# First attention products of two chunks moved into the last superchunk's LSTMs, with the pieces around them placed anew

## Chip, cores and metric

The kernel runs on one core of a Trainium2 chip, in one launch. The metric is the device time of that launch in microseconds (us). Before the change it was 1873.44 us, the median of three runs (1873.34 to 1873.54).

## What is computed

The input is x, 128 batches of 64 tokens with 256 channels, in f32. Four layers each add to x something made of relu(layernorm(x)). Layer 0 is a graph convolution with two products and batch norms. Layer 1 is two graph convolutions, and then LSTMs over windows of 1, 2, 3 and 4 tokens. Layer 2 is a causal attention with one head, layer 3 an attention with four heads and a mask. Cut to what matters here:

```python
# layer 1, with h = relu(layernorm(x))
h = relu(einsum('ts,bsh->bth', adj, h @ Wg0 + bg0))
h = relu(einsum('ts,bsh->bth', adj, h @ Wg1 + bg1))
for p in range(1, 5):                      # windows of p tokens, an LSTM over each
    last = lstm(Wih[p-1], Whh[p-1], bih[p-1], bhh[p-1], windows(h, p))
    h = h with token (p-1) of each window set to last
x = x + h
# layer 2, with h = relu(layernorm(x))
q, k, v = split(h @ Wqkv)
attn = softmax(causal(q @ k.T / 16 + adj))
x = x + (attn @ v) @ Wo
```

## The kernel before

The 8192 tokens are cut into 16 chunks of 512, and for the LSTMs two chunks make a superchunk, so there are 8 superchunks, numbered 0 to 7. The stages follow each other: layer 0; then, at `START`, the convolutions of chunks 0 and 1 with the first pieces of chunk 2; then the LSTMs of the eight superchunks one after the other; then the two attentions, chunk by chunk.

The order of the instructions on TensorE, VectorE, GpSimd and the DMA queue of SyncE (and, from the LSTMs on, on ScalarE) is the order of the program. Each engine works through its own list, and waits at an instruction until what it needs is there.

**The LSTMs.** `lstms(sc, hT)` is a generator that runs `single` (windows of one token) and then `lstm` for p = 2, 3, 4, and yields at places in between. The loop at the end of the stage counts the places: `single` ends at place 3, p = 2 takes 4 to 7, p = 3 takes 8 to 13, p = 4 takes 14 to 21; halves (4.5, 5.5) are places within a step. Each matrix product is done in seven block products, called by their kinds 1 to 7. In `single` the kinds stand in the order 2, 1, 5, 6, 3, 7, 4 for three gates each; kinds 1, 6, 7 and 4 go to the same three PSUM banks, so a product into them waits until VectorE (L1386) or ScalarE has taken the one before. The VectorE helper lines that come up again are L1386 (adds in `single`), L1378 (its new state), L1134 (adds at the start of `lstm`), L1104 (the state l_hs of a step), L298 (`add_squares`).

**What runs beside them.** At each place the loop takes the next piece of other generators, in the order in which `units` put them there:

- `convolutions(c)` for the chunks of the next superchunk, and, begun earlier still, for those of the one after it. It has 16 pieces: (1) scale, on VectorE; (2) transposes on VectorE (L1002), a store of the result to HBM, four loads of it in another order, and the load of x; (3) `add_squares`, which adds what was loaded to x; (4, 5) sums for the norm on VectorE and GpSimd; (6, 7) its application on ScalarE; (8) aggregation on TensorE; (9) two copies on VectorE; (10) the product v, 3.4 us on TensorE; (11) bound on VectorE; (12) the product u, 3.5 us on TensorE; (13) bias on VectorE; (14) aggregation; (15, 16) relu on ScalarE. Two pieces of chunk 2 run in `START`.
- `residual(c)` for the chunks of the superchunk before: transposes on VectorE (L1302) and a store; four loads; `add_squares`.
- `ahead(c)` for chunks whose residual is done: a reordering through HBM, norm, and a store of relu(layernorm(x)) for layer 2.

The tuples `FIRST` and `BEGUN` (superchunk 0), `CONV` (1 to 6), `RESIDUAL`, `LATE`, `LATEST`, `AHEAD` and `FINAL` say at which place each piece of the two chunks stands. In superchunk 0 the first tuple of `FIRST` is for chunk 2, the second for chunk 3; those of `BEGUN` are for chunks 4 and 5.

**Superchunk 7** has no convolutions beside it. Where TensorE would idle there, `IDLE` puts `keep_busy`: transposes of the identity matrix that nobody reads (L151), 54 of them in five places. At place 8 the loads of the first two chunks for layer 2 are issued.

**The attentions.** A hand-written list of steps, `FIRST` (a second variable of that name), begins them: `q2` and `v2a`, `v2b` are the first products of layer 2, `score2`, `exp2`, `divide2`, `turn2`, `out2` its attention, `keep` stores x, `norm3`, `apply3`, `chan3` make the channel-major input of layer 3, `q30` to `k31` and `v3a`, `v3b` its products, `score3` its scores. `res1` are the three pieces of `residual` and `pair1` the reordering for the last two chunks, 14 and 15, whose LSTMs have just ended. After `FIRST` come the lists `THIRD`, `ROUND`, `NORM` and `LAST`.

```python
n = -1
for mark in lstms(sc, hTs[sc]):
    n = n + 0.5 if mark else int(n) + 1
    for u in todo.pop(n, ()):
        next(u)
```

Of the kernel before, what the change touches and what calls it, by code (L numbers as in the profile page):

```python
# [8 lines left out]
F32 = mybir.dt.float32  # L9
# [10 lines left out]
def kernel(  # L20
# [841 lines left out]

    xs = {}
    w1, close_w1 = pool("w1", 1)
    l1, close_l1 = pool("l1", 2)
    l1r, close_l1r = pool("l1r", 2, "right")
    wg0_sb = w1.tile([P, KD, D], F32, name="wg0_sb")
    wg1_sb = w1.tile([P, KD, D], F32, name="wg1_sb")
    nc.sync.dma_start(wg0_sb, wg0.rearrange("(k p) f -> p k f", p=P))
# [5 lines left out]

    wih1 = w1.tile([P, 3, 7, P], F32, name="wih1")

    def load_single():

        rest = l1.tile([P, KD, CH], F32, tag="cell", name="wih1_rest", bufs=1)[:, 0, : 3 * P]  # L880
        rest = rest.rearrange("p (g f) -> p g f", g=3)
        for g, q in enumerate(GATES[:3]):
            raw = wih_t[0].rearrange("(k p) (q f) -> p k q f", p=P, f=D)[:, :, q]
            nc.sync.dma_start(wih1[:, g, 0], raw[:, 0, :P])
            nc.sync.dma_start(rest[:, g], raw[:, 0, P:])
            nc.sync.dma_start(wih1[:, g, 1:3], raw[:, 1].rearrange("p (c f) -> p c f", c=KD))
        yield
        w = wih1.rearrange("p g s f -> p s g f")
        for dst, a, b, op in ((3, rest, w[:, 2], OP.add), (4, w[:, 3], w[:, 0], OP.subtract),
                              (5, w[:, 0], rest, OP.subtract), (6, w[:, 1], w[:, 4], OP.subtract)):  # L890
            nc.gpsimd.tensor_tensor(w[:, dst], a, b, op)
        yield
# [15 lines left out]
    def scaled(y, c, m):  # L908
# [4 lines left out]
        else:  # L913
            nc.vector.tensor_scalar(y[:, m, :], z2[c][:, m, :], sc2[:, one], sh2[:, one],
                                    op0=OP.mult, op1=OP.add)

    def conv_tile(c):

        t = l1.tile([P, KD * CH], F32, tag="cv", name=f"cv_{c}", bufs=2)
        return t.rearrange("p (k n) -> p k n", k=KD), t.rearrange("p (j d) -> p j d", d=D)  # L920
# [417 lines left out]
    def single(b, name, t, ending):  # L1338
# [21 lines left out]
        def product(kind):  # L1360
            for g in range(3):
                nc.tensor.matmul(folded(ps(g, kind)), wih1[:, g, KINDS1[kind], :], right[kind],  # L1362
                                 start=kind in (2, 5, 1), stop=True, skip_group_check=True)
# [143 lines left out]

    RESIDUAL = (0, 3, 5.5), (2, 5, 8.5)
    CONV = (3, 4, 5, 5.5, 7, 8, 9, 10, 10), (5, 5, 6, 9.5, 11, 11.5, 13, 14, 15, 15.5, 17, 18, 20)
    BEGUN = (11, 11, 14.5, 17, 17, 20, 21), (17.5, 19, 21)  # L1510
    FIRST = (1, 1, 1, 2, 3, 4, 4, 5, 5.5, 7, 8, 9, 10, 10), (1, 2, 4.5, 5, 5, 6, 9.5, 11, 11.5, 13, 14, 15, 15.5, 17, 18, 20)
    AHEAD = (6, 7), (9, 10)
    LATE = (4.5, 4.5, 5.5, 9, 19.5), (9, 9.5, 11, 12, 21)
    LATEST = (4.5, 4.5, 5.5, 9, 9.5), (9.5, 9.5, 10, 11, 11.5)
    IDLE = {5: 4, 7: 18, 9: 10, 13: 14, 15: 8}
    FINAL = (6, 7, 11, 11, 12, 15, 15.5), (9, 10, 13, 13, 16, 17, 17.5)
# [25 lines left out]
    with tc.manual_schedule(engines={mybir.EngineType.PE, mybir.EngineType.DVE, mybir.EngineType.Pool,  # L1542
# [4 lines left out]
        for sc in range(last + 1):  # L1547
# [22 lines left out]
            if sc + 1 < last:  # L1570
                for i in range(SUP):
                    units(BEGUN[i], convs[(sc + 2) * SUP + i])
            n = -1
            for mark in lstms(sc, hTs[sc]):
                n = n + 0.5 if mark else int(n) + 1
                for u in todo.pop(n, ()):
                    next(u)
                if sc == last and n in IDLE:
                    keep_busy(IDLE[n], f"l{n}")
                if sc == last and n == 8:  # L1580

                    new_hT(sc + 1)
                    for c in range(SUP):
                        load2(c, hTs[sc + 1][:, c, :].rearrange("p (q n) -> p q n", q=Q))
            assert not todo
# [4 lines left out]

    w2p, close_w2 = pool("w2", 1)
    l2, close_l2 = pool("l2", 2)
    wqv_sb = w2p.tile([P, KD, 2 * D], F32, name="wqv_sb")
    nc.sync.dma_start(wqv_sb, products_far)
    wqk_sb, wvo_sb = wqv_sb[:, :, :D], wqv_sb[:, :, D:]
    w3_sb = w2p.tile([P, KD, 3 * D], F32, name="w3_sb")
    nc.sync.dma_start(w3_sb, w3.rearrange("(k p) f -> p k f", p=P))

    def project_v(dst, hT, w, first, name, pairs=range(NJ // 2)):
        for t in pairs:  # L1600
            ps = bank(f"v_{name}_{t}").rearrange("p (j d) -> p j d", d=D)
            for i in range(2):
                j = 2 * t + i
                for k in range(KD):
                    nc.tensor.matmul(ps[:, i, :], hT[:, k, j, :], w[:, k, first : first + D], start=(k == 0),  # L1605
                                     stop=(k == KD - 1))
            nc.scalar.copy(dst[:, 2 * t : 2 * t + 2, :], ps)  # L1607

    def project_t(m, hT, w, name):
        ps = bank(f"p{m}_{name}")  # L1610
        for k in range(KD):
            nc.tensor.matmul(ps.rearrange("p (a n) -> p a n", n=P), w[:, k, m * P : (m + 1) * P],  # L1612
                             hT[:, k], start=(k == 0), stop=(k == KD - 1))
        return ps


# [41 lines left out]
    for l in "23":  # L1658
# [6 lines left out]
    steps["load2"] = lambda c: load2(  # L1665
        c, l2.tile([P, Q, CH * KD // Q], F32, tag="hT2", name=f"hT2_{c}"))


    @step
    def q2(c):  # L1670
        st[c, "q2"] = q = l2.tile([P, KD, CH], F32, tag="q", name=f"q2_{c}")
        hT = st[c, "hT2"]
        nc.scalar.copy(q[:, 0, :], project_t(0, hT, wqk_sb, f"q2_{c}"))
        st[c, "q2b"] = project_t(1, hT, wqk_sb, f"q2_{c}")

# [4 lines left out]
    def v2h(c, t):  # L1680
        if not t:
            st[c, "v2"] = l2.tile([P, NJ, D], F32, tag="v", name=f"v2_{c}")
        project_v(st[c, "v2"], st[c, "hT2"], wvo_sb, 0, f"2_{c}", [t])

# [260 lines left out]

    @step
    def table(c):

        nc.scalar.activation(small.tile([P, 1], F32, tag="table", name="table"),
                             hTs[last][:, 0, :1], AF.Exp)  # L1950
# [57 lines left out]
    def store(c, t):  # L2008
# [3 lines left out]
        for r in range(2):  # L2012
# [18 lines left out]

    FIRST = """table+0 load2+2 q2+0 copyq2+0 res1+14 res1+15 v2a+0 v2b+0 score2+0 res1+14 res1+15
               exp2+0 q2+1 divide2+0 copyq2+1 load2+3 turn2+0 v2a+1 v2b+1 out2+0 keep+0 res1+14 res1+15
               score2+1 norm3+0 exp2+1 q2+2 divide2+1 copyq2+2 apply3+0 back+0 v2a+2 v2b+2 turn2+1
               score2+2 chan3+0 pair1+14 pair1+14 out2+1 keep+1 exp2+2 divide2+2 q30+0 k30+0 turn2+2
               norm3+1 pair1+15 pair1+15 q31+0 k31+0 apply3+1 out2+2 keep+2 square3+1 score3+0 norm3+2
               v3a+0 load3+1 v3b+0"""
    LAST = """exp3-2 sum3-2 load3+0 divide3-2 qa-1 q5-1 c11-1 v3a-1 qb-1 c12-1 qc-1 turn3-2 qd-1 out3-2
# [26 lines left out]
    close_l2()  # L2065
    close_w2()
    close_l3()
# [47 lines left out]
```

## Time and profile before

The page is of one profiled execution, of 1871.9 us from the first to the last instruction. The stages that the change touches, from the table of busy times by window:

| Stage | window, us | TensorE busy, us | VectorE busy, us |
|---|---|---|---|
| end of START and first half of superchunk 0 | 265 to 340 | 71.82 | 45.04 |
| rest of 0, and superchunks 1 to 6 (most) | 440 to 1360 | 915.94 | 662.40 |
| superchunk 7 | 1360 to 1505 | 138.47 | 97.37 |
| start of the attentions | 1505 to 1560 | 54.29 | 37.30 |
| end of the attentions | 1700 to 1872 | 166.23 | 123.20 |

A row of the profile's groups reads: line, engine, operation, what it writes, what it reads, size, how often; then busy time and the mean of one; then how long the engine idled just before such instructions, and who released it. The granted clock of TensorE stands beside each window: 1.00 is full speed.

The 54 transposes of `IDLE` are recorded at 0.272 us each, and overlap: 18 in a row take 2.13 us, so one takes up 0.118 us.

### The profile page before, as it was taken

The numbers are of one execution on the slowest core, as the hardware profiler recorded it, in microseconds if no ns is written. First come the engines' busy times: TensorE is split into PE (matmuls) and PEld (weight loads), VectorE is DVE, ScalarE is ACT, GpSimd is POOL, SyncE is SP. The second block draws the span as 40 slices with busy tenths as digits, with TensorE's granted clock in tenths as the row PEclk, the third lists the DMA queues.
The fourth block names the chain that finished last, engine by engine and source line by source line (L and its number), as shares of the span: only waits on it lengthen the run. The fifth ranks groups of instructions, "written<-read, shape, count | busy, mean of one in ns | idle before, by whom it ended". The sixth has DMA issues, their size and how long they took to land.

```text
span 1871.9 us, 40786 instructions
## 1 busy us (share of the span) xinstructions
PE 1839.2 (98%) x15509; PEld 1513.0 (81%) x15509; DVE 1322.3 (71%) x3410; ACT 1051.9 (56%) x2500; POOL 614.1 (33%) x856
## 2 busy tenths in 40 slices
PE   8999989999999999999999999999999999999998
PEld 6877856996997898799699689789969967777776
DVE  6768856667677667777866866876667667766776
ACT  5766635556557466565655655746555534444453
POOL 5855723223213323222322332332222214322232
PEclk9999999999999999999999999999999999999999
DMA  3223642224333333341432532342234244444433
GB/s 115 71 68 136 236 184 65 84 98 158 124 114 145 115 136 125 112 157 49 158 130 108 181 124 114 147 136 103 96 102 153 68 158 138 154 140 141 142 114 114
DMA packets 113010, 234.48 MB, mean 125 GB/s; under 512 B 11696, under 2 KB 76592, under 8 KB 112816
## 3 DMA queue, kind: packets, MB, share of 16 engines
q1 hardware_dynamic: 111920, 230.02, 36.5%
q8 instruction: 123, 2.02, 0.4%
q0 software_dynamic: 320, 1.05, 0.2%
q10 hardware_dynamic: 576, 0.82, 0.1%
q14 instruction: 71, 0.58, 0.1%
HBM read 164.21 MB, written 67.63 MB: 124 GB/s over the span
## 4 chain that ended last, share of the span: by engine, by line
PE 83%; DVE 9%; ACT 3%; POOL 2%; issue 1%; DMA 1%; SPq 0%; DVEq 0%; ACTq 0%; POOLq 0%
PE x L1180 22%; PE z L1180 11%; PE y L1180 5%; PE v L1605 5%; PE y L1127 4%; PE u L943 3%; PE v L929 3%; PE p_q L1612 3%; PE x L1362 3%; PE y L1362 3%; PE X L1801 3%; PE x L1127 2%; PE X L437 2%; PE X L513 2%; PE z L1127 1%
## 5 line engine op out<-in xcount | busy, mean ns | idle before, releaser
L1095 ACT ACTIVATE l_gates<-l_gates,bias 128x256 f32<-128x256 f32 (+4 forms) x528 | 238.1, 498 | 211.9 <-DVE l_gates L1189 110.1
L1180 PE MATMUL x<-xd,wset 128*128 128x128 f32 (+2 forms) x1152 | 255.0, 303 | 0.2 <-ACT l_gates L1186 0.2
L1180 PE MATMUL x<-l_hd,wset 128*128 128x128 f32 (+2 forms) x1152 | 254.5, 303 | 0.0
L1246 POOL TENSOR_TENSOR l_gates<-l_gates 128x512 f32<-128x512 f32 (+2 forms) x48 | 75.2, 1567 | 386.4 <-ACT l_gates L1095 386.4
L1189 DVE TENSOR_TENSOR l_gates<-l_gates,z 128x128 f32<-128x128 f32 (+2 forms) x384 | 102.5, 319 | 130.8 <-PE z L1180 128.8
L1180 PEld LDWEIGHTS x<-xd,wset 128*128 128x128 f32 x1152 | 187.7, 191 | 5.9 <-issue 0.5
L1180 PEld LDWEIGHTS x<-l_hd,wset 128*128 128x128 f32 x1152 | 187.8, 191 | 5.0
L1189 DVE TENSOR_TENSOR l_gates<-l_gates,x 128x128 f32<-128x128 f32 (+2 forms) x384 | 121.3, 321 | 91.9 <-PE x L1180 88.2
L1180 PE MATMUL z<-l_hs,wset 128*128 128x128 f32 (+2 forms) x768 | 147.2, 304 | 3.7 <-DVE l_hs L1104 3.7
L1180 PE MATMUL z<-hT,wset 128*128 128x128 f32 (+2 forms) x768 | 146.2, 303 | 0.0
L1186 ACT COPY l_gates<-y 128x128 f32<-128x128 f32 (+2 forms) x192 | 53.1, 290 | 137.3 <-PE y L1180 130.7
L1180 PEld LDWEIGHTS z<-l_hs,wset 128*128 128x128 f32 x768 | 116.8, 191 | 9.4 <-DVE l_hs L1104 6.1
L1180 PEld LDWEIGHTS z<-hT,wset 128*128 128x128 f32 x768 | 117.1, 191 | 3.3
L1095 ACT ACTIVATE l_gates<-x,bias 128x128 f32<-128x128 f32 (+2 forms) x216 | 84.9, 393 | 30.8 <-PE x L1180 28.1
L1180 PE MATMUL x<-hT,wset 128*128 128x128 f32 (+2 forms) x384 | 85.9, 305 | 0.0
L1180 PE MATMUL x<-l_hs,wset 128*128 128x128 f32 (+2 forms) x384 | 84.8, 303 | 0.0
L327 POOL TENSOR_TENSOR xd<-hT 128x128 f32<-128x128 f32 (+2 forms) x72 | 42.8, 594 | 128.1 <-DVE hT L1106 100.0
L1180 PE MATMUL y<-l_hd,wset 128*128 128x128 f32 (+2 forms) x384 | 83.5, 310 | 0.3 <-DVE l_hd L327 0.2
L1180 PE MATMUL y<-xd,wset 128*128 128x128 f32 (+2 forms) x384 | 81.9, 305 | 0.9 <-ACT l_gates L1095 0.6
L1620 POOL TENSOR_TENSOR s<-s,mx 128x256 f32<-128x256 f32 (+2 forms) x33 | 40.4, 1226 | 128.4 <-DVE mx L1619 120.6
L1261 ACT ACTIVATE l_gates<-l_cell 128x256 f32<-128x256 f32 (+2 forms) x144 | 55.2, 383 | 42.9 <-DVE l_cell L1260 42.9
L1607 ACT COPY v<-v 128x512 f32<-128x512 f32 x64 | 37.1, 582 | 71.2 <-PE v L1605 71.1
(350 smaller groups left out, 4588.4 us busy)
## 6 DMA issues: line engine op xcount, KB each, us to landing
wset<-wfar SPq DMA_DIRECT2D x96, 896.0 KB, 6.9
hT<-far_h SPq DMA_DIRECT2D x124, 128.0 KB, 3.2
far_h<-hm SPq DMA_DIRECT2D x16, 512.0 KB, 3.0
far_n<-xs SPq DMA_DIRECT2D x16, 512.0 KB, 3.9
xs<-far_n SPq DMA_DIRECT2D x64, 128.0 KB, 3.8
far_x<-xs SPq DMA_DIRECT2D x16, 512.0 KB, 2.9
x<-far_x SPq DMA_DIRECT2D x64, 128.0 KB, 3.2
xt<-in_x_dram SPq DMA_DIRECT2D x15, 512.0 KB, 3.9
```

The lines of the kernel that those rows point to most:

```text
L929: nc.tensor.matmul(banks[m], wg0_sb[:, k, m * P : (m + 1) * P], agg[:, k, :], start=(k == 0), stop=(k == KD - 1))
L943: nc.tensor.matmul(banks[j // 2][:, j % 2, :], v[:, k, j * P : (j + 1) * P], wg1_sb[:, k, :], start=(k == 0), stop=(k == KD - 1))
L1095: nc.scalar.activation(gate(q, c, part), src, AF.Tanh if q == 2 else AF.Sigmoid, bias=bs[:, q * KD + c : q * KD + c + 1])
L1127: nc.tensor.matmul(folded(self.psum(kind)), wsets[p, self.q][:, BLOCKS[kind][0], :], ox[0][kind], start=kind in (1, 5), stop=True, skip_gr ...
L1180: nc.tensor.matmul(folded(self.psum(kind)), wsets[p, self.q][:, BLOCKS[kind][i], :], (ox[self.s] if part == "x" else oh)[kind], start=firs ...
L1189: nc.vector.tensor_add(gate(self.q, *dst), gate(self.q, *a), self.psum(kind))
L1246: nc.gpsimd.tensor_mul(gates[:, 0, :, :n], gates[:, 0, :, :n], gates[:, 2, :, :n])
L1261: nc.scalar.activation(gate(2, c, part), cells[:, c, part], AF.Tanh)
L1362: nc.tensor.matmul(folded(ps(g, kind)), wih1[:, g, KINDS1[kind], :], right[kind], start=kind in (2, 5, 1), stop=True, skip_group_check=True)
L1605: nc.tensor.matmul(ps[:, i, :], hT[:, k, j, :], w[:, k, first : first + D], start=(k == 0), stop=(k == KD - 1))
L1612: nc.tensor.matmul(ps.rearrange("p (a n) -> p a n", n=P), w[:, k, m * P : (m + 1) * P], hT[:, k], start=(k == 0), stop=(k == KD - 1))
L1801: nc.tensor.matmul(st[c, tag][:, i * CH // 2 : (i + 1) * CH // 2].rearrange("p (a n) -> p a n", n=P), w, st[c, "o7"][kind], start=first an ...
```

## The change

It does three things, which belong together.

1. The first products of layer 2 for chunk 0 (`q2`, `v2`) and chunk 1 (`q2`) are made in superchunk 7, in a new generator `begin_attention` with eight pieces at the places `EARLY`, in place of most of the filler transposes. Of these 8 remain, at a new place, 11. `FIRST` of the attentions loses those steps and is ordered anew.
2. For that, weights and some buffers must live longer than the LSTM stage. A pool `lasting` holds `wg0_sb` and `wg1_sb` (which are loaded anew with the products of layer 2's weights at place 0 of superchunk 7), two chunk-sized buffers `cv`, and four of the seven blocks of `wih1`, whose room then serves v of chunk 0, and after it the weights of layer 3, `w3_sb`, now loaded by a step `weights3`.
3. Pieces are placed anew: those of the residual, and the first late piece of the norm, one place later; those of superchunk 0 spread over later places, with a tuple of its own, `BEGUN_FIRST`, for the chunks begun there.

```diff
-    wg0_sb = w1.tile([P, KD, D], F32, name="wg0_sb")
-    wg1_sb = w1.tile([P, KD, D], F32, name="wg1_sb")
+    wg0_sb = lasting.tile([P, KD, D], F32, name="wg0_sb")
+    wg1_sb = lasting.tile([P, KD, D], F32, name="wg1_sb")
...
+    def begin_attention():
+
+        tiles = [shared(f"{n}2_0") for n in ("hT", "q")]
+        for w, i in ((wg0_sb, 0), (wg1_sb, 1)):
+            nc.sync.dma_start(w, products_far[:, :, i * D : (i + 1) * D])
+        load2(0, tiles[0].rearrange("p (q n) -> p q n", q=Q))
...
+        yield
+        for m in range(KD):
+            nc.scalar.copy(st[0, "q2"][:, m, :], project_t(m, st[0, "hT2"], wg0_sb, "q2_0"))
+            yield
+        for t in range(NJ // 2):
+            project_v(st[0, "v2"], st[0, "hT2"], wg1_sb, 0, "2_0", [t])
+            yield
+        new_hT(last + 1)
+        load2(1, hTs[last + 1][:, 1, :].rearrange("p (q n) -> p q n", q=Q))
+        st[1, "q2"] = hTs[last + 1][:, 0, :].rearrange("p (k n) -> p k n", k=KD)
+        yield
+        for m in range(KD):
+            nc.scalar.copy(st[1, "q2"][:, m, :], project_t(m, st[1, "hT2"], wg0_sb, "q2_1"))
+            yield
+
-    RESIDUAL = (0, 3, 5.5), (2, 5, 8.5)
+    EARLY = 0, 3, 5, 7, 9, 9, 13, 15
+    RESIDUAL = (0, 4, 5.5), (3, 5, 9)
     CONV = (3, 4, 5, 5.5, 7, 8, 9, 10, 10), (5, 5, 6, 9.5, 11, 11.5, 13, 14, 15, 15.5, 17, 18, 20)
     BEGUN = (11, 11, 14.5, 17, 17, 20, 21), (17.5, 19, 21)
-    FIRST = (1, 1, 1, 2, 3, 4, 4, 5, 5.5, 7, 8, 9, 10, 10), (1, 2, 4.5, 5, 5, 6, 9.5, 11, 11.5, 13, 14, 15, 15.5, 17, 18, 20)
+    BEGUN_FIRST = (12, 14.5, 17, 19, 19, 20, 21), (20, 21, 21)
+    FIRST = (1, 3, 3, 4, 4.5, 5, 5.5, 7, 8, 9, 9.5, 11, 11.5, 11.5), (2, 5, 8.5, 9, 9.5, 10, 11, 13, 14, 15, 15.5, 17, 17.5, 19, 20, 20)
     AHEAD = (6, 7), (9, 10)
-    LATE = (4.5, 4.5, 5.5, 9, 19.5), (9, 9.5, 11, 12, 21)
+    LATE = (4.5, 4.5, 5.5, 9, 19.5), (9.5, 9.5, 11, 12, 21)
     LATEST = (4.5, 4.5, 5.5, 9, 9.5), (9.5, 9.5, 10, 11, 11.5)
-    IDLE = {5: 4, 7: 18, 9: 10, 13: 14, 15: 8}
+    IDLE = {11: 8}
...
-                    units(BEGUN[i], convs[(sc + 2) * SUP + i])
+                    units((BEGUN if sc else BEGUN_FIRST)[i], convs[(sc + 2) * SUP + i])
+            if sc == last:
+                units(EARLY, begin_attention())
...
-    FIRST = """table+0 load2+2 q2+0 copyq2+0 res1+14 res1+15 v2a+0 v2b+0 score2+0 res1+14 res1+15
-               exp2+0 q2+1 divide2+0 copyq2+1 load2+3 turn2+0 v2a+1 v2b+1 out2+0 keep+0 res1+14 res1+15
-               score2+1 norm3+0 exp2+1 q2+2 divide2+1 copyq2+2 apply3+0 back+0 v2a+2 v2b+2 turn2+1
-               score2+2 chan3+0 pair1+14 pair1+14 out2+1 keep+1 exp2+2 divide2+2 q30+0 k30+0 turn2+2
-               norm3+1 pair1+15 pair1+15 q31+0 k31+0 apply3+1 out2+2 keep+2 square3+1 score3+0 norm3+2
-               v3a+0 load3+1 v3b+0"""
+    FIRST = """table+0 load2+2 score2+0 res1+14 v2a+1 v2b+1 res1+15 exp2+0 score2+1 divide2+0 q2+2 copyq2+2
+               exp2+1 turn2+0 divide2+1 load2+3 v2a+2 v2b+2 out2+0 keep+0 weights3+0 res1+14 res1+15 turn2+1
+               norm3+0 score2+2 out2+1 keep+1 res1+14 res1+15 exp2+2 apply3+0 back+0 divide2+2 chan3+0
+               pair1+14 pair1+14 turn2+2 q30+0 k30+0 norm3+1 pair1+15 pair1+15 out2+2 keep+2 q31+0 k31+0
+               apply3+1 square3+1 score3+0 norm3+2 v3a+0 load3+1 v3b+0"""
```

## The prediction

> **What bounds it now.** I read the busy shares first, then a table by stage, then the gaps of TensorE one by one. The page:
>
> ```profile
> PE 1839.2 (98%) x15509; PEld 1513.0 (81%) x15509; DVE 1322.3 (71%) x3410; ACT 1051.9 (56%) x2500; POOL 614.1 (33%) x856
> PE 83%; DVE 9%; ACT 3%; POOL 2%; issue 1%; DMA 1%; SPq 0%; DVEq 0%; ACTq 0%; POOLq 0%
> ```
>
> TensorE (PE) is busy 98% and carries 83% of the chain that ended last: a microsecond counts if TensorE idles, or runs dummy transposes, less. The table by stage (PE busy is the second number after the window):
>
> ```profile
> 265.00:340.00 75.00, 71.82 (x441) 49.80 (x440) 45.04 (x96) 40.00 (x80) 19.12 (x23) 0.98 0.25 86
> 440.00:1360.00 920.00, 915.94 (x6871) 783.97 (x6870) 662.40 (x1839) 545.27 (x1424) 261.17 (x374) 1.00 0.36 124
> 1360.00:1505.00 145.00, 138.47 (x887) 121.88 (x886) 97.37 (x292) 83.07 (x222) 37.90 (x59) 1.00 0.32 99
> 1505.00:1560.00 55.00, 54.29 (x492) 36.86 (x491) 37.30 (x90) 23.63 (x45) 14.67 (x19) 1.00 0.58 178
> ```
>
> So 3 us of idle lie in the first superchunk (265 to 340), 4 in the six middle ones, 6.5 in the last (1360 to 1505), and under 1 in the start of the attention. Where, the timeline of PE shows (start, duration, work, in brackets the idle before it and who ended it):
>
> ```profile
> 293.26 4.51 PE L1362 MATMUL x<-xd,wih 128*128 128x512 f32 x6 [2.34 <-DVE l_gates L1386]
> 606.91 1.10 PE L1127 MATMUL y<-hT,wset 128*128 128x256 f32 x4 [0.20 <-DVE hT L1378]
> 656.39 1.41 PE L1180 MATMUL z<-l_hs,wset 128*128 128x168 f32 x8 [0.42 <-DVE l_hs L1104]
> 1406.07 2.13 PE L151 MATMUL idle_l<-ident 128*128 128x128 f32 x18
> ```
>
> The first is one hole; the next two recur in each middle superchunk; the last is a filler, 0.118 us a transpose. Who bounds the start of the attention, the chain of waits tells:
>
> ```profile
> 1516.74 0.12 issue
> 1516.88 0.29 issue
> 1517.17 0.57 DVE xs L1729
> 1517.77 2.49 DVE xs L298 x4
> ...
> 1524.76 0.08 DVE nmr_n L185
> 1524.89 0.48 issue
> 1525.37 1.57 ACT h L187 x3
> 1526.94 0.95 ACT v L1607 x2
> 1527.88 0.28 ACT att L1643
> 1528.21 1.10 PE o L1726 x32
> ```
>
> PE looks full here, but from 1516.7 to 1528 the chain runs through VectorE (DVE) and ScalarE: PE is only just covered. That is the line I trust most.
>
> **The Trainium skill.** (1) "TensorE: Matmul & The Clock Gate", Part 1: the array's clock is halved after an idle window of about 3.4 us and restored after a busy one. The trace agrees: after the 2.34 us hole the granted clock is 0.50 from 293.3 to 296.7, and six matmuls took 4.34 us instead of 2.57 (+1.7). (2) Same page, "Architectural detail": "ACT/DVE are strict FIFO". Here too: the 2.34 us hole is an add behind ten queued pieces of convolution. (3) "DMA: Bandwidth & Descriptors", "Anatomy of one DMA": a fixed cost of about 2 us, mostly the receipt of the last byte. The trace: a 512 KB store of `ym` lands 2.6 to 4.3 us after issue, a 128 KB load of it about 3.1.
>
> **First superchunk, inside.** At place 1 DVE loses eight norm operations and two scalings (287.61 to 290.64, 3.1 us), so the add at 290.64 is in time: the hole (2.34) and the slow window (1.7) go, -4.1. But what filled PE at places 4, 5, 13 (1.1, 3.4, 3.4 us) comes at 5, 7, 15. The last superchunk, which has no convolutions, shows the bare holes: 2.1 us at 3 to 4 (some of it from transposes that aren't here: I take 1.2), 1.9 at 5 (0.5 of filler, 0.59, 0.81) against 1.1 us of aggregation, 1.9 at 13 against 1.1; 0.5 more where eight norm operations stand before the first adds of place 3. New waits 1.2+0.8+0.8+0.5 = 3.3. Sum -0.8 (-2.5 to +1.5).
>
> **First superchunk, its end.** BEGUN_FIRST gives chunk 5 the places (20, 21, 21), where BEGUN had (17.5, 19, 21): the transposes of piece 2 and the add of piece 3 now stand next to each other on DVE, and between them lies a round trip through HBM. Now: DVE ends the LSTM's tail at 435.4; transposes 1.2 (436.6); store lands +2.9 (439.5); four loads at 0.43 apart, landing 3.1 (444.4); the load of `xs` behind them, 2.9 to 5.0 (445 to 447). Four weight loads of 896 KB, issued 429.4 to 432.8, keep the DMA engines full to about 438. So add_squares runs at 446.2 to 447.5 and the first L1386 add ends at 448.1. Behind that add waits PE: its products 2, 1, 5 of the next superchunk last from 431.97 to 439.69 (three times 2.57), and the fourth needs a bank which this add frees. Stall 448.1-439.7 = 8.4 us (6.5 to 10), plus a halved clock once (1.7; 0.8 to 2.6): +10.1.
>
> **Middle superchunks.** The transposes of the second residual (2.05 us) leave place 2, its add place 8.5, for 3 and 9; the norm piece goes from 9 to 9.5. The add's 1.28 us stood right in front of the l_hs product that PE waits for by 0.42; the transposes in front of the state it awaits by 0.20. DVE has idle time for them where they go: 1.30 us at 609, 2.65 at 662. -0.62 in six superchunks: -3.7, I take -3.5.
>
> **Last superchunk.** Out: 46 of 54 fillers (5.4 us). In: q of chunks 0 and 1 (8 records, 3.44 us each, from 1499.96 to 1503.40) and v of chunk 0 (3.54): 10.4 us in pieces of 1.73 to 1.77. They stand in the fillers' places and in 6.1 us of waits, so nearly all is hidden; pieces too long for their hole, and 8 fillers at place 11 where no hole was: +0.7 (-0.5 to +2). Loads and ScalarE's six copies (0.57 each) lie beside it.
>
> **Start of the attention.** PE has 10.4 us less. Count from the last LSTM matmul (1499.96). PE: scores 0 1.1, v1 3.5, scores 1 1.1, q2 3.5: 9.3; the turn of chunk 0 waits for DVE (tail 3.3, scores 0.85, two residual transposes 4.1, scores 0.85, divide 1.0: 10.2); v2 to 14.0, output 0 to 15.1, turn, scores 2, output 1: 17.5. Next on PE is chunk 0's chan3, which needs its norm; on DVE, in order after output 0: its add (16.4), norm sums 2.2, scores 0.85, add of output 1 1.25 (20.7), add_squares of chunks 14 and 15 2.5, nmr: 23.3 at best. It was 24.8. But the loads for those add_squares, before at 1509 to 1512, now follow output 0's store (issued 16.4) and a new 786 KB load of w3 on the queue: issued 17.2 to 20.7, landing 3.2 later behind 1.3 MB: about 22.4 and 24.2; nmr 25.6. So chan3 ends at 28.6 (before 27.8), PE idle about 9 us before it. After it 14.1 us to the end of FIRST (14.4 before: output 1 is gone, but output 2 no longer covers the copy of k, 0.85), plus a slow window 1.7: 44.4 against 42.2, +2.2 (-1.1 to +6). The 10.4 us come back as idle time.
>
> **Sum.** -0.8 + 10.1 - 3.5 + 0.7 + 2.2 = +8.7: 1882.1 us. The rest of the attention is bound by PE (166.23 of 172 us busy after 1700) and only shifts.
>
> **Rivals.** *PE stays the bound of the attention's start.* For: under 1 us idle there now, 30% of DVE free. Against: the DVE chain above. Then -10.4 in place of +2.2: 1869.5, and 1859.4 if the round trip is hidden too. Faster; 0.10. *The round trip hides behind work that I overlook at the border.* Then 10.1 goes: 1872.0, no change; 0.13. Against it: PE has 7.7 us of work, the trip takes 9. *Both stalls at their long end* (12.6 and 6, slow windows twice): about 1889; 0.17. My forecast has 0.60.
>
> So faster 0.10, same 0.13, slower 0.77. The range leaves out the faster rival and most of the second, and takes in the long end: 1876 to 1889.
>
> **What would show it.** After: a PE gap of 6 to 10 us near 438, ended by a DVE l_gates add behind the two xs adds of L298, with the clock at 0.5 after it; no 2.34 us hole at 291; no 0.42 and 0.20 in the middle superchunks; a gap of 7 to 10 us some 18 us after the last LSTM matmul, ended by ACT h. It is wrong if PE runs through 439 without a gap, or if chan3 starts 18 us after the last LSTM matmul.

## The result, and the profile after

The changed kernel takes **1900.9 us** (median; 1900.6 to 1902.0) against 1873.5 before (1873.3 to 1873.7): a ratio of 1.0147, 95% interval 1.013 to 1.0165. It is slower, as forecast, but by 27.4 us where 8.7 were forecast, and outside the range.

The first page of the changed kernel, busy shares and chain:

```profile
PE 1840.9 (97%) x15463; PEld 1513.1 (80%) x15463; DVE 1319.9 (70%) x3408; ACT 1053.2 (55%) x2502; POOL 611.6 (32%) x856
PE 83%; DVE 6%; ACT 5%; POOL 2%; issue 1%; DMA 1%; SPq 0%; DVEq 0%; ACTq 0%; POOLq 0%
```

TensorE was busy 1839.2 us before and is busy 1840.9 now, in a span that grew from 1871.9 to 1898.9. So 25 of the 27 us are idle time, which grew from 32.7 to 58.0 us; the other 1.7 are busy time, with fewer filler transposes in it and more matmuls at half clock. The table by stage says where to look; the columns are the window, its length, busy time of PE, PEld, DVE, ACT and POOL, then the mean granted clock, the DMA share and GB/s:

```profile
448.00:485.00 37.00, 27.86 (x146) 16.64 (x145) 23.09 (x42) 18.80 (x37) 9.86 (x11) 0.86 0.31 89
...
1526.00:1574.00 48.00, 35.59 (x313) 21.14 (x311) 27.23 (x69) 14.14 (x26) 7.62 (x11) 0.86 0.55 172
```

At the border of the first two superchunks (448 to 485) 9.1 us are idle, in the start of the attention (1526 to 1574) 12.4, both at a mean clock of 0.86. Four waits of PE name the holes, and their lines stand below: 11.84 us in front of L240 (for ACT, L187), 8.65 in front of L1369 (for VectorE, L1393), 4.48 in front of L228 (for ACT, L210) and 4.44 in front of L228 (for ACT, L187). The first two were forecast, the third was thought to be small, and the last was not in the forecast at all. Lines of the LSTMs stand 7 further down than before, those of the attentions 24; the products of the attentions are now L1521 and L1528 (L1605 and L1612 before). To give each its share I took the starts of the same matmuls in both traces; each stage is the difference of two of them:

| stage (first matmul to first matmul) | before | after | difference | forecast |
|---|---|---|---|---|
| START: first transposes `at_b` to first LSTM product | 28.29 | 32.54 | +4.25 | none |
| first superchunk, p=1 | 23.66 | 19.39 | -4.27 | -4.1 |
| first superchunk, p=2 to 4 | 134.37 | 144.01 | +9.64 | +3.3 |
| second superchunk, p=1 (the border) | 19.21 | 29.96 | +10.75 | +10.1 |
| from there to the last superchunk | 898.37 | 899.43 | +1.06 | -3.5 |
| last superchunk | 150.30 | 150.87 | +0.57 | +0.7 |
| last LSTM product to first product of the next list (THIRD) | 42.34 | 47.33 | +4.99 | +2.2 |

(Before, the second superchunk begins at 432.0 us, so the window 440 to 1360 of the earlier table holds nothing of superchunk 0.)

**START.** PE's gap, then SyncE's queue, before and after:

```profile
253.93 2.39 PE L228 MATMUL agg_b<-adjt_bd,cv 64*64 64x64 f32 x64 [4.44 <-ACT cv L187]
```

```profile
232.62 0.93 SPq L961 DMA_DIRECT2D early<-in_x_dram  x2
...
244.54 1.31 SPq L968 DMA_DIRECT2D early<-in_x_dram  x2
```

The input of chunks 0 and 1 (`early`) was issued at 232.6 us before and is issued at 244.5 now. No instruction of this stage was edited. But the new pool `lasting` holds `cv`, 8 KB per partition, ahead of the LSTM pool, so `early` (16,384 bytes) now begins at byte 158,816 of a partition in place of 150,624. Before, it reached only into `wqkv_sb`, which PE reads until 232.3. Now its end also lies on `wo_sb` (170,176 to 172,224), which PE reads until 243.7, and on the staged copy of wg1 (173,248 to 175,296), which PE reads last, until 244.5:

```profile
243.48 1.03 PE L752 MATMUL c<-wg_st,c 128*128 128x256 f32 x4
```

The load goes out when that has ended, and VectorE's first add stands idle for 5.98 us in front of it.

**The hole at place 1** is gone: twelve products run without the 2.34 us between them.

```profile
292.12 5.31 PE L1369 MATMUL x<-xd,wih 128*128 128x512 f32 x12
```

**The border** is as drawn in the prediction. SyncE's queue first, then VectorE, then PE, before and after:

```profile
445.94 0.32 SPq L261 DMA_DIRECT2D far_y<-ym  x1
449.28 1.97 SPq L268 DMA_DIRECT2D cv<-far_y  x4
```

```profile
455.78 1.29 DVE L298 TENSOR_TENSOR xs<-xs,cv 128x512 f32<-128x512 f32 x2 [9.87 <-DMA xs<-in_x_dram]
```

```profile
439.69 2.74 PE L1362 MATMUL x<-xd,wih 128*128 128x512 f32 x6
...
457.82 4.67 PE L1369 MATMUL x<-xd,wih 128*128 128x512 f32 x6 [8.65 <-DVE l_gates L1393]
```

VectorE sits idle 9.87 us between the transposes (444.6 to 445.9) and the add, for the round trip through HBM; what lands last is the load of x, which stands behind the four loads in the queue. PE sits idle behind it for 8.65; six products then take 4.67 us, where six take 2.74 to 2.81 at full clock. Before, the trip had left the queue by 429.3, and PE did not wait. In each middle superchunk PE now waits 0.49 to 0.70 us at the start of p=2, where it had waits of 0.20 and 0.42 before.

**Place 5 of the first superchunk**: PE before (where this aggregation stood at place 4) and after, then POOL and ACT.

```profile
300.56 1.16 PE L228 MATMUL agg_b<-adjt_bd,cv 64*64 64x64 f32 x64
...
314.27 1.20 PE L228 MATMUL agg_b<-adjt_bd,cv 64*64 64x64 f32 x32 [4.48 <-ACT cv L210]
```

```profile
305.06 0.73 POOL L330 TENSOR_TENSOR xd<-hT,xd 128x256 f32<-128x256 f32 x1
...
307.19 0.20 POOL L202 TENSOR_TENSOR nmr_b<-mv_b,rstd_b 128x4 f32<-128x4 f32 x1
```

```profile
307.76 1.09 ACT L210 ACTIVATE cv<-xs,nmr_b,rstd_b 128x256 f32<-128x256 f32 x2 [6.16 <-POOL nmr_b L203]
...
313.63 1.09 ACT L210 ACTIVATE cv<-xs,nmr_b,rstd_b 128x256 f32<-128x256 f32 x2
```

The norm of chunk 2 was moved to place 3. Its sums are ready at 302.7 on VectorE, but its root is on POOL, behind seven differences `xd` of p=2 (300.7 to 305.8), and with POOL's own four steps behind them the last of it comes at 307.7. ACT, which takes its work in order, stands idle for 6.16 us in front of L210, with the LSTM's own activations (L1102) behind it. Its second half, at place 4.5, runs after those, and PE stands in front of the aggregation.

**Start of the attention**: PE before and after, then the chain of waits there.

```profile
1526.99 0.76 PE L240 MATMUL tc_n<-ident,h 128*128 128x128 f32 x5 [0.16 <-ACT h L187]
...
1550.88 2.80 PE L240 MATMUL tc_n<-ident,h 128*128 128x128 f32 x8 [11.84 <-ACT h L187]
```

```profile
1538.37 5.87 DMA w_sb<-in_w_dram
1544.25 4.38 DMA hT<-far_h
...
1548.82 1.29 DVE xs L298 x2
```

The residual's loads stand behind `w_sb` (the weights of layer 3) in the queue; two adds that nothing on PE needs at this point wait for them, and the norm that PE does need waits behind the adds.

### The profile page after: what moved, and what is told of

Same layout as the page of the kernel before. It is cut to its first block, busy times and chain, and to the rows that moved or that the text cites. A ratio compares the mean times of both kernels' runs of the same rounds, so it can differ in the third digit from the quotient of the medians.

```text
span 1898.9 us, 40682 instructions
## 1 busy us (share of the span) xinstructions
PE 1840.9 (97%) x15463; PEld 1513.1 (80%) x15463; DVE 1319.9 (70%) x3408; ACT 1053.2 (55%) x2502; POOL 611.6 (32%) x856
## 4 chain that ended last, share of the span: by engine, by line
PE 83%; DVE 6%; ACT 5%; POOL 2%; issue 1%; DMA 1%; SPq 0%; DVEq 0%; ACTq 0%; POOLq 0%
PE x L1187 22%; PE z L1187 11%; PE v L1521 6%; PE y L1187 6%; PE y L1134 4%; PE v L936 3%; PE u L950 3%; PE p_q L1528 3%; PE X L1825 3%; PE X L437 2%; PE x L1134 2%; PE X L513 2%; PE x L1369 2%; PE y L1369 2%; PE Y L1825 1%
## 5 line engine op out<-in xcount | busy, mean ns | idle before, releaser
L1102 ACT ACTIVATE l_gates<-l_gates,bias 128x256 f32<-128x256 f32 (+4 forms) x528 | 238.1, 498 | 213.8 <-DVE l_gates L1196 111.8
L1102 ACT ACTIVATE l_gates<-x,bias 128x128 f32<-128x128 f32 (+2 forms) x216 | 84.7, 392 | 31.1 <-PE x L1187 28.4
L1369 PE MATMUL x<-xd,wih 128*128 128x512 f32 x144 | 66.6, 609 | 8.9 <-DVE l_gates L1393 8.7
```

Source lines behind the costliest of these rows:

```text
L1102: nc.scalar.activation(gate(q, c, part), src, AF.Tanh if q == 2 else AF.Sigmoid, bias=bs[:, q * KD + c : q * KD + c + 1])
L1369: nc.tensor.matmul(folded(ps(g, kind)), single_block(KINDS1[kind])[:, g, :], right[kind], start=kind in (2, 5, 1), stop=True, skip_group_c ...
```

## The experiments

The stages in what follows are those of the table. Each kernel starts from the changed one unless it says otherwise.

### 1. The border's add at another place

```diff
-    BEGUN_FIRST = (12, 14.5, 17, 19, 19, 20, 21), (20, 21, 21)
+    BEGUN_FIRST = (12, 14.5, 17, 19, 19, 20, 21), (20, 21)
...
+                    if sc == 1 and i:
+                        units([4], convs[SUP * 2 + 1])
```

> The changed kernel (1900.9 us) with one piece moved: the first add_squares of chunk 5 (DVE add after the HBM round trip) runs at place 4 of the second superchunk, where it cannot stand ahead of the first LSTM adds, in place of place 21 of the first. Theory: the whole border stall (PE idle 8.65 us at 457.8 plus the slow window after it, together 10.7 us against the kernel before) hangs on this one DVE add in the queue; gone to within 1.5 us: 1890.2 us (1889.5 to 1892). Rival A: the stall is there because the transposes and weight loads of that border come late in any case and PE would wait for something else (the copies of the banks, the stores): under half of it goes, above 1895.5. Rival B: the add waits for its data at the new place too and stalls PE there: no change, 1899 or more.

Measured: 1891.5 us (1890.9 to 1892.3), ratio 1.0093 (1.0078 to 1.0108). The border's stage is 19.2 us again, as before: the whole 10.75 hung on this one add. One step was off: place 4 turned out to be still ahead of the first adds of p=2, behind 2.1 us of transposes of the residual and 1.2 of copies, so part came back there. VectorE, then PE:

```profile
465.69 2.05 DVE L298 TENSOR_TENSOR xs<-xs,cv 128x512 f32<-128x512 f32 x2
```

```profile
468.22 2.05 PE L1134 MATMUL y<-xd,wset 128*128 128x256 f32 x4 [2.47 <-DVE l_gates L1141]
```

### 2. The first inputs on memory that is free early

```diff
         wqkv_sb = stage.tile([P, KD, 3 * D], F32, name="wqkv_sb")
+        pad = stage.tile([P, 1280], F32, name="pad")
         wo_sb = stage.tile([P, KD, D], F32, name="wo_sb")
```

> The changed kernel (1900.9 us) with one unused SBUF tile of 5 KB per partition placed in front of wo_sb, so that the tile early (input of chunks 0 and 1) lies again on memory that is read for the last time at 232 us, not 244 us. No instruction is changed. Theory: the input load is issued at about 232.6 in place of 244.5, the DVE add of L979 runs at about 246.4, the 4.44 us gap of PE at 253.9 and the slow clock after it go: -4.2 us, 1896.7 (1896 to 1897.6). Rival: the weight products that end at 244 and the loads of the first LSTM weights bound this stretch anyway, or the wait is only handed on to the weight loads behind in the queue: within 1 us of 1900.9.

Measured: 1899.75 us (1897.8 to 1901.4). Locally the theory holds to the figure: the load goes out at 232.66, START takes 28.6 us in place of 32.5, and 3.8 us are still won at the end of the first superchunk. But the border's stage grew from 29.96 to 32.4, and the attention's from 47.3 to 48.0:

```profile
455.70 5.39 PE L1370 MATMUL x<-xd,wih 128*128 128x512 f32 x6 [10.34 <-DVE l_gates L1394]
```

The store of `ym` took 5.6 us until its loads could be issued, 3.3 in the changed kernel and 3.2 to 3.6 in runs 3 to 5. The profiled execution is the slowest of the four (1901.4), and the median is 1.1 us below the changed kernel, with ranges that overlap: no gain is shown, where 4.2 were expected. A gain ahead of a stall on a transfer need not come out behind it; it had to be tried again without the stall (run 10).

### 3. The second half of the norm ahead of the activations

```diff
-    FIRST = (1, 3, 3, 4, 4.5, 5, 5.5, ...
+    FIRST = (1, 3, 3, 4, 4, 5, 5.5, ...
```

> The changed kernel (1900.9 us) with the second half of chunk 2's application (ACT L210) at place 4 of the first superchunk in place of 4.5: ahead of the LSTM's activations of that half place. Theory: the aggregation at place 5 no longer waits 4.48 us for ACT, and the slow window after it (1.7 us) goes; 0.3 to 1.2 us of wait stay: 1895.4 us (1894.7 to 1896.6). Rival: the first half waits for POOL's nmr at 307.7 anyway and the LSTM's activations, pushed back by 1.1 us, make PE wait as long elsewhere: 1899.5 or more.

Measured: 1900.8 us (1900.5 to 1901.3), no change. PE's gap at this point:

```profile
312.90 0.67 PE L1187 MATMUL y<-xd,wset 128*128 128x256 f32 x2 [2.60 <-ACT l_gates L1102]
```

The aggregation is in time, and PE waits 2.60 us for the LSTM's activations one step later, since POOL's root still comes at 307.7. p=2 to 4 cost 7.8 us more than before in place of 9.6; the rest was lost again at the border (+11.2) and in a longer half-clock window at the attention (17.1 us, 13.7 in the changed kernel). The rival was right: the place of the second half alone is not the cause. What is left is the late root; runs 6 and 9 move it.

### 4. The residuals' loads first

```diff
-  load2+3 v2a+2 v2b+2 out2+0 keep+0 weights3+0 res1+14 res1+15 turn2+1
+  load2+3 res1+14 res1+15 v2a+2 v2b+2 out2+0 keep+0 weights3+0 turn2+1
```

> The changed kernel (1900.9 us) with the second pieces of the last two residuals (the 8 loads of hT) issued right behind the loads for chunk 3 of the attention, ahead of the stores and the weights of layer 3 in the queue. Theory: the loads go out at about 1534 in place of 1538.9 to 1544.6, the two add_squares run at 1542 to 1544.5 in place of 1546.7 and 1548.8, chan3 of chunk 0 starts at about 1545.3 in place of 1550.9: -5.5 us, 1895.4 (1894 to 1897). Rival A: PE is short of work at this point whatever the loads do (its products were moved ahead), so the idle is only moved to the next wait (copies of k, output 2): 1899.5 or more. Rival B: the store and w3 behind the loads come late and stall q30: 1901 or more.

Measured: 1896.7 us (1895.5 to 1897.7), ratio 1.0121 (1.0106 to 1.0136).

```profile
1545.55 2.80 PE L240 MATMUL tc_n<-ident,h 128*128 128x128 f32 x8 [6.12 <-ACT h L187]
```

The gap falls from 11.84 to 6.12, the stage from 47.3 to 40.9 us. Half of the gap was the queue. Of the 6.4 us 1.7 are lost again behind this stage, up to the end.

### 5. Output 0 ahead of the products of chunk 2

```diff
-  load2+3 v2a+2 v2b+2 out2+0 keep+0 weights3+0 res1+14 res1+15 turn2+1
-  norm3+0 score2+2 out2+1 keep+1 res1+14 res1+15 exp2+2 apply3+0 back+0 divide2+2 chan3+0
+  load2+3 res1+14 res1+15 out2+0 keep+0 v2a+2 v2b+2 weights3+0 turn2+1
+  norm3+0 apply3+0 score2+2 out2+1 keep+1 exp2+2 back+0 chan3+0 divide2+2 res1+14 res1+15
```

> The changed kernel (1900.9 us) with the list of the attention's first steps put in another order: the residuals' loads right behind the loads of chunk 3 (alone that gave 1896.7), output 0 ahead of the 3.6 us of v of chunk 2, the application of the norm of chunk 0 ahead of scores 2 and output 1, and the two residual adds behind chan3 of chunk 0. Theory: the 11.84 us gap is no lack of work but a DVE chain that starts late, since output 0 stands behind v of chunk 2 on PE, and that carries adds which nothing on PE needs; with both mended, chan3 starts 17 to 19 us after the last LSTM product with a wait under 2 us and no slow window, and the stretch from the last LSTM product to the first product of the next list takes 33 to 35 us (47.2 in the changed kernel, 42.3 before): 1888 us (1886 to 1890). Rival: the norm's own chain (add, sums, POOL's root, ACT) is what PE waits for, so that only the adds' 2.5 us more than in the run with early loads are won: 1893 to 1895.

Measured: 1896.7 us (1895.6 to 1899.4). The order does what it should: chan3 starts 18.0 us after the last LSTM product, with no gap over 0.5 us ahead of it. But the stage takes 40.2 us, not 33 to 35, for a new wait stands behind it: `w_sb` still goes out at 1538.4, behind eight loads and a store in the queue, lands 2.93 us after PE wants it, and PE is at half clock from 1543.3 to 1550.1. Nothing is won over run 4, so neither expectation came true.

```profile
1546.16 3.75 PE L1528 MATMUL p_q<-hT,w_sb 128*128 128x512 f32 x4 [2.93 <-DMA w_sb<-in_w_dram]
```

### 6. The norm at places 1 and 2

```diff
-    FIRST = (1, 3, 3, 4, 4.5, 5, ...), (2, 5, ...)
+    FIRST = (1, 1, 2, 4, 4.5, 5, ...), (3, 5, ...)
...
+                        units([4.5], convs[SUP * 2 + 1])
```

> The run with the add at place 4 (1891.5 us) with that add at place 4.5, behind the first adds of p=2, and in the first superchunk the norm pieces of chunk 2 at places 1 and 2 in place of 3 and 3, and chunk 3's scaling at 3 in place of 2. Theory: ACT stood idle from 301.5 to 307.7 us in front of L210, because POOL computed that norm's root and nmr only behind eight differences xd of p=2 that are queued ahead of place 3; with the norm at 1 and 2 it comes ahead of them, the LSTM's activations are no longer held up, and the 4.48 us wait in front of the aggregation with its slow window goes (-5 to -6.5), as does the 2.47 us wait at the start of p=2 in the second superchunk with its slow window (-2.5 to -3.5): 1883 us (1881.5 to 1885). Rival: more DVE work at places 1 and 2 opens the hole of 2.34 us and its slow window of the kernel before again: 1886.5 or more.

Measured: 1891.45 us (1888.3 to 1893.1). Its second half came out: with the add at 4.5 the border's stage is 19.2 us and nothing is lost at p=2. The first half failed: p=2 to 4 of the first superchunk cost 13.2 us more than before, where they cost 9.6 in the changed kernel. PE:

```profile
301.90 1.39 PE L1134 MATMUL z<-xd,wset 128*128 128x256 f32 x4 [2.09 <-POOL xd L327]
316.70 1.20 PE L228 MATMUL agg_b<-adjt_bd,cv 64*64 64x64 f32 x32 [2.72 <-ACT cv L210]
```

Now the root stands ahead of `xd` on POOL and waits for VectorE until 298.7, so that the first `xd` starts at 300.7 (296.3 in the changed kernel), late for PE; and the second half of the application, still at 4.5, still stands behind the LSTM's activations.

### 7. The old places of the first superchunk

```diff
-    FIRST = (1, 3, 3, 4, 4.5, 5, 5.5, ...
+    FIRST = (1, 1, 1, 2, 3, 4, 4, ...
...
-                    units((BEGUN if sc else BEGUN_FIRST)[i], convs[(sc + 2) * SUP + i])
+                    units(BEGUN[i], convs[(sc + 2) * SUP + i])
```

> The changed kernel (1900.9 us) with the places of the first superchunk's pieces as before (the old FIRST, and BEGUN in place of BEGUN_FIRST); all else stays. Theory: by the comparison of the traces the new places of the first superchunk cost 9.6 (places 4 to 21) and 10.75 (border) and win 4.3 (up to p=2): -16.1 us, 1884.8 (1883 to 1887). Rival A: the border alone is to blame, and the wait at place 5 only takes the place of one that the old places would have with the new allocation: about 1890. Rival B: the products moved to the last superchunk and the attention's new order cost most: 1893 or more.

Measured: 1884.9 us (1883.75 to 1886.05), ratio 1.0058 (1.0045 to 1.0072), as expected to 0.1 us. In its trace the two stages of the first superchunk and the border take 23.7, 134.0 and 19.2 us, as before the change, with the new allocation and the moved products still there. So the new places of the first superchunk cost 16 of the 27 us, and neither the allocation nor the products have a part in them.

### 8. Residual and norm pieces one place later, alone

From the kernel before:

```diff
-    RESIDUAL = (0, 3, 5.5), (2, 5, 8.5)
+    RESIDUAL = (0, 4, 5.5), (3, 5, 9)
-    LATE = (4.5, 4.5, 5.5, 9, 19.5), (9, 9.5, 11, 12, 21)
+    LATE = (4.5, 4.5, 5.5, 9, 19.5), (9.5, 9.5, 11, 12, 21)
```

> The kernel before (1873.5 us) with the new RESIDUAL and LATE alone: the second residual's transposes at place 3 and its add at 9, the norm piece behind it at 9.5. Theory now: the two waits of 0.20 and 0.42 us in each middle superchunk go, but the 2.1 us of transposes stand with 1.25 us of copies ahead of the first adds of p=2, where PE then waits 0.5 to 0.7: no gain, 1874.3 us (1873 to 1875.5). Rival, as predicted: DVE's idle time takes them for nothing: 1870 (1869.5 to 1871).

Measured: 1873.1 us (1872.7 to 1874.0), ratio 0.9996 (0.9988 to 1.0004): no difference that can be told, inside the expected range and not the -3.5 of the prediction. From the end of the border to the last superchunk it takes 898.3 us, 898.4 before. In a middle superchunk PE's one wait is now

```profile
610.75 1.10 PE L1127 MATMUL y<-xd,wset 128*128 128x256 f32 x4 [0.49 <-DVE l_gates L1134]
```

(0.49 to 0.70 in the six), which takes the place of the two (0.20 and 0.42).

### 9. The whole norm at place 1, both halves ahead of the activations

With the border's add at 4.5 as in run 6:

```diff
-    FIRST = (1, 3, 3, 4, 4.5, 5, ...
+    FIRST = (1, 1, 1, 3, 4, 5, ...
```

> The changed kernel (1900.9 us) with the add of chunk 5 at place 4.5 of the second superchunk (in the last run that took the border's 10.75 us to zero without a new wait) and, in the first superchunk, both norm pieces of chunk 2 at place 1 and its two halves of application at 3 and 4, ahead of the LSTM's activations of place 4.5. Theory: the 9.6 us of places 4 to 21 hang mostly on one jam, in which the norm's POOL part is queued behind the differences xd and ACT stands behind it; a norm at place 2 pushed the differences back instead, and a half at 4.5 stood behind five activations. With this order neither happens: places 4 to 21 cost 3 to 4 us in place of 9.6, the hole at place 1 (2.34 before, with the scaling of chunk 3 in the queue as well) is 1 us: 1885 us (1883.5 to 1887). Rival: the aggregation at place 5 rather than 4 is itself what costs, since PE has nothing else in place 4, so that the wait only moves: 1888 or more.

Measured: 1884.5 us (1884.0 to 1885.5), ratio 1.0059 (1.0044 to 1.0075), inside the expectation. ACT no longer waits for POOL in front of L210 (the first half; the second follows at 304.3):

```profile
301.71 1.08 ACT L210 ACTIVATE cv<-xs,nmr_b,rstd_b 128x256 f32<-128x256 f32 x2
```

p=2 to 4 cost 4.3 us more than before in place of 9.6, p=1 wins 2.6 in place of 4.3. So the jam on POOL and ACT is over half of the 9.64, of which 1.7 are paid at p=1: 3.7 us net. The run moves the root and both halves at once and doesn't part POOL's queue from ACT's order. Of the 4.3 that stay, six waits of PE (0.71, 0.63, 0.85, 0.52, 0.23 and 0.42) are 3.4; what each hangs on was not tried.

### 10. All that helped, together

The old places (7), the unused tile (2), and:

```diff
+  exp2+1 turn2+0 divide2+1 load2+3 out2+0 weights3+0 keep+0 res1+14 res1+15 v2a+2 v2b+2 turn2+1
+  norm3+0 apply3+0 score2+2 out2+1 keep+1 exp2+2 back+0 chan3+0 divide2+2 res1+14 res1+15
```

> The changed kernel (1900.9 us) with the old places of the first superchunk (alone 1884.9), the unused tile of 5 KB that lets the first inputs load early, and the attention's first steps in this order: output 0 and the load of w3 ahead of the stores, the residuals' loads behind them, v of chunk 2 behind output 0, the norm's application ahead of scores 2, the residual adds behind chan3. Theory: the old places leave nothing that absorbs a gain, so START's 4.2 us count in full now (in the run with the unused tile they were given back in a longer border stall); in the attention w3 no longer lands 2.9 us late and chan3 follows output 1 directly: 35 us from the last LSTM product to the next list's first product, where before has 42.3 and the changed kernel 47.2: 1873.5 + 0.3 (START) + 1 (middle and last superchunks) - 7 (attention) = 1867.8 us (1866 to 1870.5), faster than before. Rival A: the transfers (2.1 MB within 15 us) only trade places, and the residual adds or q30 wait for them: 1871 to 1874. Rival B: START's gain is absorbed here too: 1872.

Measured: **1871.4 us** (1868.8 to 1874.6), ratio 0.9989 (0.9983 to 0.9996): 2.1 us faster than before, 29.5 faster than the changed kernel. START takes as long as before (28.29), so its 4.25 us were the allocation and nothing else. The start of the attention takes 35.1 us, as expected, 7.2 less than before, and PE runs from chan3 into q without a wait for `w_sb`:

```profile
1521.48 1.88 PE L1529 MATMUL p_q<-hT,w_sb 128*128 128x512 f32 x4
...
1544.63 0.67 PE L1826 MATMUL Z<-hT,w_sb 128*128 128x256 f32 x2 [1.46 <-DMA hT<-far_h]
```

The last line is part of what the sum had not: up to the end of the kernel 2.6 us are given back after this stage, 1.7 of them up to this wait. The profiled execution was the fastest of 21 (1868.8); the median lies 2.5 above it.

### 11 and 12. Two attempts at that wait

```diff
-  norm3+1 pair1+15 pair1+15 out2+2 keep+2 q31+0 k31+0 apply3+1 square3+1 score3+0
+  norm3+1 pair1+15 pair1+15 out2+2 keep+2 apply3+1 square3+1 q31+0 k31+0 score3+0
```

> The run mended (1871.4 us) with the application of chunk 1's norm and its transposes (apply3, square3) ahead of the second halves of q and k of chunk 0 in the attention's first steps. Theory: in mended the stretch up to the next list took the 35 us that were expected, and 1.7 us were given back behind it, where PE waits 1.46 us for hT of chunk 1: its nmr stands on DVE behind the copy of k (1530.4, while POOL's root was there at about 1527.2), so its store and its loads come 3 us late. With it 3 us earlier this wait goes in every run, and the scatter of mended (1868.8 to 1874.6) shrinks: 1869.5 us (1868 to 1871). Rival: the scatter and the give-back are those of the transfers in the later rounds, which this doesn't touch, or the copies of q and k that now stand behind four activations on ACT stall the scores of layer 3: 1871 to 1873.

Measured: 1871.3 us (1869.9 to 1873.2), ratio 0.9987 (0.9981 to 0.9994), the same as mended. The transposes came earlier, the store did not: it stands in the queue behind four loads of another chunk that wait for their own store. And PE now waits 1.23 us for the copy of k on VectorE.

```profile
1533.84 1.71 SPq L279 DMA_DIRECT2D xs<-far_n  x4
...
1536.12 1.68 SPq L261 DMA_DIRECT2D far_h<-mid  x1
```

So those loads were put behind the store:

```diff
-  norm3+1 pair1+15 pair1+15 out2+2 keep+2 q31+0 k31+0 apply3+1 square3+1 score3+0
+  norm3+1 out2+2 keep+2 q31+0 k31+0 apply3+1 square3+1 pair1+15 pair1+15 score3+0
```

> The run mended (1871.4 us) with both pieces of pair1 of chunk 15 (a store and four loads behind it in the queue) put behind the store of chunk 1's transposes (square3). In the run before this one the transposes came 3 us earlier and the store didn't: it stood in the queue behind these loads, which wait for their own store to land. Theory: the store goes out at about 1533.7 in place of 1535.0 to 1536.6 and the loads of hT at about 1536.8 in place of 1540.0; the 1.46 us wait of PE for them goes: 1869.8 us (1868.5 to 1871). Rival: the loads of hT are bound by something behind the store (the engines' share, the loads of load2), or the late pairs are awaited in turn: 1871 or more.

Measured: 1873.3 us (1869.7 to 1875.2), ratio 0.9997 (0.9988 to 1.0005): no gain over mended and likely a loss, though the two intervals overlap. The store goes out at 1534.0, as expected, but the four loads now stand between it and the loads of `hT`, wait for their own store until 1540, and PE waits 3.15 us in place of 1.46. What would take this wait away is open.

## Why the prediction was right and wrong

**Direction and two mechanisms: right.** The border: the add waits for a round trip, 8.65 us on PE against 8.4, and 10.75 in all against 10.1; run 1 shows that it is the whole of it. The hole at place 1 went, -4.27 against -4.1. The last superchunk costs 0.57 against 0.7, but that is in part luck: in the trace of run 8 the shift of the residual alone takes 0.75 off this stage, which the forecast did not count there. If the two effects add up, the products and fillers cost 1.3.

**START: a term was missing.** The prediction went through lists of places and passed over the line that opens a pool. It has a cost: +4.25 (runs 2 and 10). The step would have been to ask, for each tile behind the new pool, what lay on its bytes before, and who reads that last. Before, the load went out at 232.6 and was needed at 246.4. "DMA: Bandwidth & Descriptors", "Anatomy of one DMA", in the Trainium skill is written for DMAs that GpSimd issues, but says of DMA engines in general that they do not wait on semaphores: any such wait happens on the issuing sequencer. The trace agrees for SyncE, which issued nothing from 232.1 to 244.5. (The queue stood still as long in the kernel before, from 234.1 to 244.8, but with `early` already on its way.)

**Inside the first superchunk: the term "new waits 3.3" was mis-sized; it is 9.64.** The step that failed is the wait at place 5, put at 0.8: it is 4.48 us, with 1.7 more from half clock after it. The prediction charged the moved norm with its VectorE operations alone ("0.5 more where eight norm operations stand before the first adds of place 3") and put its other parts at nothing: the root on POOL, behind 5.1 us of differences, and the application on ACT, which takes it in order. The rule "ACT/DVE are strict FIFO", which the prediction quotes, was applied to VectorE only. Run 9 shows that this jam is 5.3 of the 9.64 us.

**Middle superchunks: "DVE has idle time for them where they go" failed.** -3.5 was forecast; the shift alone gave -0.8 (the interval is -2.2 to +0.7), and by its trace nothing of that in the middle superchunks. The idle time of VectorE at 609 and 662 was real, but the transposes went in front of the first adds of p=2, which PE awaits: 0.49 to 0.70 came for 0.62. The +1.06 of the changed kernel goes with the border's stall: without it (runs 6, 7 and 9) this stage takes 898.4 to 898.6 us.

**Start of the attention: mechanism right, two terms too small.** The eight loads were put at 17.2 to 20.7 us after the last LSTM product; they were issued from 17.3 on but took 5.70 us, and the second add began at 27.3 in place of 24.2. And the idle time of 11.84 us came with 13.65 us of half clock, of which PE worked through 6.4: 3.2 us lost, where one window, 1.7, was counted. +4.99 against +2.2.

Together: 4.25 (START), 6.2 (9.64 - 4.27 against -0.8), 4.6 (middle), 2.8 (attention) and 0.65 (border), less 0.1, are 18.3 of the 18.8 us missed. The range took in long ends for the stalls that were seen and nothing for those that were not.

**And the products themselves?** Of their 10.4 us, 7.2 come off the start of the attention once the chain there is in order (run 10), 2.6 are given back behind it, and the last superchunk pays 0.3; the median run keeps 2.1 in all. The new order alone, without moving products, was not run. By the trace of before it could win little in that stage: PE stands idle there for 0.7 of the 42.3 us.

## What to carry to other kernels

When work is spread over places in a fixed order, follow each piece through all engines that it touches, in their queues; a norm with a root on a third engine is not a VectorE piece. A new pool or a tile that moves is an edit: ask what lay on its bytes and when that is read last. Where a stall hangs on a transfer, gains ahead of it may not come out behind it, so test them again once the stall is gone.

## What the runs showed of the hardware

- The granted clock falls in whole windows: apart from the last stretch, which the end of the trace cuts off, 3.41, 6.83, 10.24, 13.65 and 17.07 us are all that the traces of these kernels have. That fits the free-running window of 3413 ns that "TensorE: Matmul & The Clock Gate", Part 1, "What's actually happening", states. What I had not expected is the length: in the changed kernel the clock stayed at half for 6.83 us after 4.44 us idle, for 3.41 after 4.48, and for 13.65 around the 11.84 us gap.
- The prediction names that page for a clock that is halved after an idle window of about 3.4 us, and takes its 2.34 us hole for agreement. In this point it is none, for less was enough: 2.34 us in the kernel before, 2.34 to 2.35 in runs 7, 8 and 12, 2.09 in run 6. In the 3.41 us just ahead of the halving PE was still busy for 1.07 us in the kernel before and for 1.32 in run 6.
- The same gap brings different clocks: the hole at place 1 brought one half-clock window in the kernel before and in runs 7, 8 and 12, and none in runs 10 and 11, where it is as long. In the sum it made no difference: in runs 10 and 12, which are alike up to there, the first superchunk takes 157.7 us with and without the window, because at full clock PE waits 1.70 us for ScalarE right behind it. So this is not the source of the 6 us of scatter of run 10, which stays open.
- The store of `ym`, 512 KB, held back its loads by 5.6 us in one trace and by 3.2 to 3.6 in four others, with the same work around it.
